# Macaron block on one core: ScalarE sums the last 128 queries of every second group in the score bank

## The chip, the cores and the metric

The kernel runs on one core of a Trainium2 chip. The metric is device time in microseconds of that core, from the start of the program to its end. Before the change it was 814.96 us (median of 3 runs, 813.83 to 816.62).

## The reference

Sixteen sequences of 512 tokens with 128 features (fp32) pass through a half feed-forward step, an attention, and a second half feed-forward step, each with a layer norm in front and a residual around it:

```
x = x + 0.5 * ffn(layernorm(x))
x = x + attn(layernorm(x))
x = x + 0.5 * ffn(layernorm(x))
```

The feed-forward is linear: a 128x128 weight rounded to int4 steps, a bias, and a low-rank term. The attention has 16 heads; keys and values come from a latent of 32 features, and the query weights are folded with the key weights, so each head's score is a product over 32 features. It is causal, with a softmax over the keys:

```
attn = softmax(where(key <= query, q @ k / 8, -inf))
y = attn @ v;  out = y @ Wout
```

## The kernel before, in words

Heads are worked on in groups of four (32 features each fill 128 partitions), four groups a sequence; two groups g and g + 1 form a pair. There are 32 pairs, each of five steps: STEP lists for each step a kind and, for kinds 0 and 1, which group of the pair it is for. Kind 0 is the last 128 queries (against 512 keys), kind 1 the third 128 queries with the first, kind 2 the second 128 queries of both groups. The last step of a pair is kind 0 of the odd group, g + 1.

A step n of the main loop (line 975) is a *burst* on TensorE (`burst`, line 673 on): it makes scores `sx` (queries on partitions) for the current pair, into two tiles of two PSUM banks each, and, six steps behind (LAG), transposed scores `tx` (keys on partitions) for the pair before, into four single banks. The `sx` are only there to find each query's maximum: DVE reduces them (`find_maxima`, lines 642 and 646, to `nmax`). POOL splits the maxima into three bf16 terms (lines 719 to 723), TensorE turns them (`mt`), ScalarE writes them out as `rows` (line 730), and TensorE adds them to the `tx`. ScalarE then takes the exponentials from `tx` to `pt` (line 655), and POOL zeroes what the mask forbids (line 668).

`merge` interleaves two streams of matmuls by their length: the first half of a burst writes two of the `tx` banks and the first `sx` tile, the second half the other two and the second `sx` tile. PSUM has eight banks: `ps_t` rotates over four single ones, `ps_s` over two double ones. After a burst, other products take the next single banks (`take`): the value products `o` (`values`, copied by ScalarE to `osb`, line 773), the sums `s`, the turned maxima, the query products `qt_ps` and so on. The next burst takes the banks after these.

The softmax's denominators need sums over keys, which lie on partitions of `pt`. POOL first adds the key blocks of a group (`add_01` line 738, `add_2` line 743, `add_23` line 748: b01 holds query blocks 1 to 3 without their last part, b23 that of block 3); TensorE multiplies with ones (`sum_products`, `s` from `pt` and from the two `b` tiles); ScalarE copies `s` to `ssb` (line 787). Four transfers of 2 KB take the four heads' rows of 512 sums to DRAM, one brings them back spread over 128 partitions (line 792), DVE takes reciprocals (line 822), and further transfers (lines 824 and 827) bring them back repeated over 32 partitions as `rb`, with which POOL scales `osb` (line 830).

Transfers nearly all go through SyncE's queue, in program order. All engines work in program order; the order is written out by hand. `plan` puts the pieces of the generators `front` (first feed-forward, layer norm, transposed activations, keys `kt`, queries `qt` of a sequence two or three windows ahead) and `tail` (output product, second feed-forward) at steps listed in FRONT_STEPS, SECOND_STEPS, THIRD_STEPS, FOURTH_STEPS and TAIL_STEPS, relative to the sequence's window of ten steps; a fraction says whether a piece stands before the burst (.5), after it (.75, written -.25) or at the step's end (whole).

Of the kernel before, what the change touches and what calls it, by code (L numbers as in the profile page):

```python
# [11 lines left out]
F32 = mybir.dt.float32  # L12
BF16 = mybir.dt.bfloat16
AF = mybir.ActivationFunctionType
# [11 lines left out]
def macaron_kernel(  # L26
# [331 lines left out]
    def to_dram(src, name):  # L358

        there = dram.tile([L, D], F32, tag=f"blocks_{name[0]}", name=f"blocks_{name}", bufs=2)  # L360
        nc.sync.dma_start(there.rearrange("(t p) d -> p t d", p=P), src)
        return there
# [58 lines left out]
    def front(b, st):  # L421


        x_sb, z = xs.pop(b), zs.pop(b)
        na, nb = f"a{b}", f"b{b}"
        la = ln_of("a", b) if b > 2 else early["a", b]
        lb = ln_of("b", b) if b > 1 else early["b", b]
        ln_stats(x_sb, la, "a", (0, 1))
        yield
        ln_stats(x_sb, la, "a", (2, 3))  # L430
        if b > 1:
            yield
        if 0 < b < B - 1:
            xs[b + 1] = load_x(b + 1)
            zs[b + 1] = load_blocks(x[b + 1], f"a{b + 1}")
        yield
        if b == 0:
            xt = turn(x_sb, na, "xt_a")
            yield
        xb = with_bias(x_sb, na, nc.gpsimd if b > 1 else nc.vector)  # L440
        yield
        if b:
            xt = turn_blocks(z, na, "xt_a")
            yield
        x1 = st["x1"] = ffn(xt, la, xb, na, "x1", 5)
        yield
        ln_stats(x1, lb, "b", (0, 1))
        yield
        ln_stats(x1, lb, "b", (2, 3))
        yield  # L450
        xn = ln_scale(x1, nb, lb)
        if b:
            there = to_dram(xn, nb)
            yield
            z = load_blocks(there, nb)
        yield
        xnt = turn_blocks(z, nb, "xnt_b") if b else turn(xn, nb, "xnt_b")
        yield
        mp = take(f"kt_ps_{b}")
        kt = st["kt"] = act2.tile([P, L], F32, tag="kt", name=f"kt_{b}", bufs=3)  # L460
        if b == 0:
            product(mp, wkv4_flat, xnt)
            nc.vector.tensor_copy(kt, mp)
        else:

            for j in range(NT):
                nc.tensor.matmul(
                    mp[ts(j, LD), :P], lhsT=wkv4_flat[:, :LD], rhs=xnt[:, ts(j, P)], start=True, stop=True,
                    skip_group_check=True,
                )  # L470
            kt4 = act2.tile([P, P], F32, tag="kt4", name=f"kt4_{b}", bufs=1)
            nc.vector.tensor_copy(kt4, mp[:, :P])
            yield
            kt_d = dram.tile([P, P], F32, tag="kt_d", name=f"kt_d_{b}", bufs=2)
            nc.sync.dma_start(kt_d, kt4)
            yield
            for h in range(HG):
                nc.sync.dma_start(
                    kt[ts(h, LD), :].rearrange("c (j n) -> c j n", j=NT), kt_d.rearrange("(j c) n -> c j n", j=NT)
                )  # L480

        def query(g):
            mp = take(f"qt_ps_{b}_{g}")
            product(mp, wqk_flat[:, ts(g, P)], xnt)
            if g % 2 == 0:
                st["qt", g] = act2.tile([P, 2, L], F32, tag="qt", name=f"qt_{b}_{g}", bufs=4)
            nc.scalar.copy(st["qt", g - g % 2][:, g % 2, :], mp)  # L487

        yield
        query(0)  # L490
        yield
        query(1)
        yield
        query(2)
        yield
        query(3)
        yield
# [8 lines left out]

    FRONT_STEPS = (-31, -30.5, -29, -28, -21, -19.25, -16, -16, -13, -10.5, -8, -4.25, -4, -3.5, -2, -1, 3, 4)
    SECOND_STEPS = (-9.5, -8.5, -7, -5.5, -5, -4.25, -4, -3.5, -2, -1, 3, 4)  # L510
    THIRD_STEPS = (-18.5, -18.5, -18.5, -18, -17.5, -17.25, -16, -16) + FRONT_STEPS[8:]
    FOURTH_STEPS = (-27, -26, -25.5, -25) + FRONT_STEPS[4:]
    TAIL_STEPS = (1.75, 2.5, 2.75, 3.5, 4.5, 7, 7, 7.75, 10.5)
    NORMALISED_STEPS = (5, 6)

    def tail(b, st, late=False):


        x2 = io.tile([P, NT, D], F32, tag="x2", name=f"x2_{b}")
        nm = f"c{b}"  # L520
        ln = ln_tile(nm) if late else ln_of("c", b)
        for half in (0, 1):
            yp = take(f"yp_{b}_{half}")[:, : 2 * D]
            for t in (0, 1):
                for g in range(NG):
                    product(yp[:, ts(t, D)], st["ot"][:, g, ts(2 * half + t, P)], wvo[:, g, :],
                            t == 0 and g == 0, g == NG - 1)
            nc.vector.tensor_tensor(
                x2[:, ts(half, 2), :], yp.rearrange("p (t d) -> p t d", d=D), st["x1"][:, ts(half, 2), :], ALU.add
            )  # L530
            if half and not late:
                there = to_dram(x2, nm)
            yield
            ln_stats(x2, ln, "c", (2 * half, 2 * half + 1))
            yield
        if late:
            xt = turn(x2, nm, "xt_c")
            yield
            ln_rstd(ln, "c")
            yield  # L540
            ln_newton(ln, "c")
        else:
            z = load_blocks(there, nm)
            yield
        xb = with_bias(x2, nm, nc.gpsimd)
        yield
        if not late:
            xt = turn_blocks(z, nm, "xt_c")
            yield
        x3 = ffn(xt, ln, xb, nm, "x3", 3)  # L550
        if not late:
            yield
        nc.sync.dma_start(out[b].rearrange("(t p) d -> p t d", p=P), x3)
        yield
# [80 lines left out]
    def find_maxima(sx, st, g, kind, u, pair):  # L635
# [9 lines left out]
        else:  # L645
            nc.vector.tensor_reduce(  # L646
                nmax[:, 1, heads, :], sx.rearrange("p k (u n) -> p k u n", u=2), AX.X, ALU.max, negate=True
            )

    def exponentials(tx, st, g, kind, u, pair):  # L650

        pt = probabilities(st, g + (u if kind < 2 else 0), kind)
        if isinstance(tx, list):
            for k in range(2):
                nc.scalar.activation(  # L655
                    pt[:, :, 2 * pair + k, :], tx[k].rearrange("p (b n) -> p b n", n=P), AF.Exp
                )
        else:
            nc.scalar.activation(
                pt[:, :, ts(pair, 2), :].rearrange("p b k n -> p k b n"),  # L660
                tx.rearrange("p k (b n) -> p k b n", n=P), AF.Exp,
            )
# [10 lines left out]
    def burst(n, s_at, t_at):  # L673
# [16 lines left out]
        for k in range(2):  # L690
            find_maxima(ss[k], *s_at, *s_kind, 1 - k)
            if t_at:
                exponentials(tt[k], *t_at, *t_kind, k)
        if n % STEPS == STEPS - 1:
            maxima(*s_at)
        if t_at:
# [34 lines left out]

    def add_01(st, g, k):

        if k == 0:
            st["b01", g] = probs.tile([P, 3, HG, P], F32, tag="b01", name=f"b01_{st['b']}_{g}")
        flat = [t.rearrange("p b k n -> p (b k n)")[:, ts(k, 6 * P)] for t in (
            st["b01", g], st["pt", 0, g][:, 1:], st["pt", 1, g][:, 1:])]
        nc.gpsimd.tensor_tensor(*flat, ALU.add)  # L738

# [4 lines left out]

    def add_23(st, g, u):

        both = st["b23", g + u] = probs.tile([P, HG, P], F32, tag="b23", name=f"b23_{st['b']}_{g + u}")
        nc.gpsimd.tensor_tensor(both, st["pt", 2, g][:, 2 + u], st["pt", 1, g + u][:, 0], ALU.add)  # L748

# [25 lines left out]
    def sum_products(st, g, u, s_ps):  # L775
        g1, w = g + u, ones_f[:, :LD]
        blocks(s_ps[:, :P], w, st["pt", 0, g1][:, :1], start=True)
        blocks(s_ps[:, P:], w, st["b01", g1])
        blocks(s_ps[:, 384:], w, st["b23", g1].unsqueeze(1))

    def sums(st, g, u):

        b, g1 = st["b"], g + u
        s_ps = take(f"s_{b}_{g1}")
        sum_products(st, g, u, s_ps)
        ssb = act2.tile([P, L], F32, tag="ssb", name=f"ssb_{b}_{g1}", bufs=3)
        nc.scalar.copy(ssb, s_ps)
        sums_d = dram.tile([HG, L], F32, tag="sums", name=f"sums_{b}_{g1}")
        for h in range(HG):
            nc.sync.dma_start(sums_d[h : h + 1], ssb[h * LD : h * LD + 1, :])  # L790
        st["sums", g1] = small.tile([P, HG * L // P], F32, tag="sum", name=f"sum_{b}_{g1}")
        nc.sync.dma_start(st["sums", g1], sums_d.rearrange("h n -> (h n)").rearrange("(p n) -> p n", p=P))

# [79 lines left out]
    early["a", 2] = early["b", 1]  # L873
    first, second = front(0, states[0]), front(1, states[1])
    masks()
    wmax = largest_of_rows()
    next(first)
    next(first)
# [95 lines left out]

    for n in range(N * STEPS):
        parts(n - 0.5)
        ready_work(n)
        burst(n, at(n), at(n, LAG))
        if due(n, 8):
# [124 lines left out]
```

## Time and profile before

| | |
|---|---|
| median of 3 runs | 814.96 us |
| the profiled execution's own time | 814.67 us |
| its span in the profile | 812.9 us |
| granted TensorE clock, mean | 0.989 |
| exponentials `pt`, 128x512 (ScalarE) | 616, mean 598 ns |
| maxima `nmax` of 128x1024 (DVE) | 128 on line 642, mean 1223 ns |
| POOL's add of 128x768 and of 128x512 (lines 738, 748) | 1821 ns and 1277 ns |
| POOL, busy | 678.4 us (83%) |

The profile is one execution. Its page gives busy times of the engines, the chain of work that ended last, and groups of instructions by line with a mean duration. The timeline lists instructions in order of time (start, duration, engine, line, what it writes and reads, how many); the waits list which engine waited for which, in total, how often and the longest. Matmul rows overlap each other: the distance from one start to the next says what a matmul costs TensorE.

### The profile page before, as it was taken

The numbers are of one execution on the slowest core, as the hardware profiler recorded it, in microseconds if no ns is written. First come the engines' busy times: TensorE is split into PE (matmuls) and PEld (weight loads), VectorE is DVE, ScalarE is ACT, GpSimd is POOL, SyncE is SP. The second block draws the span as 40 slices with busy tenths as digits, with TensorE's granted clock in tenths as the row PEclk, the third lists the DMA queues.
The fourth block names the chain that finished last, engine by engine and source line by source line (L and its number), as shares of the span: only waits on it lengthen the run. The fifth ranks groups of instructions, "written<-read, shape, count | busy, mean of one in ns | idle before, by whom it ended". The sixth has DMA issues, their size and how long they took to land.

```text
span 812.9 us, 35716 instructions
## 1 busy us (share of the span) xinstructions
PE 786.7 (97%) x15400; PEld 506.9 (62%) x15400; DVE 618.6 (76%) x1317; ACT 488.9 (60%) x971; POOL 678.4 (83%) x676
## 2 busy tenths in 40 slices
PE   7899999999999999999999999999999999999986
PEld 5456566675666657666566766666666766666554
DVE  7787887978779687877869787777878677686716
ACT  1237675757567565756667566666757566575651
POOL 1018898998998999898989989898999989998991
PEclk9989999999999999999999999999999999999998
DMA  5123122232422323332232323223222222212111
GB/s 138 27 57 68 32 72 60 69 71 73 95 61 69 77 66 80 76 82 60 70 84 61 84 69 82 67 67 88 56 64 67 51 72 69 59 46 59 41 41 30
DMA packets 171022, 54.01 MB, mean 66 GB/s; under 512 B 119512, under 2 KB 162680, under 8 KB 170864
## 3 DMA queue, kind: packets, MB, share of 16 engines
q1 hardware_dynamic: 170096, 51.44, 27.1%
q8 instruction: 120, 1.97, 1.0%
q14 instruction: 38, 0.31, 0.1%
q10 hardware_dynamic: 768, 0.30, 0.1%
HBM read 37.90 MB, written 13.80 MB: 64 GB/s over the span
## 4 chain that ended last, share of the span: by engine, by line
PE 75%; POOL 7%; DVE 7%; ACT 4%; DMA 4%; issue 2%; SPq 1%; DVEq 0%; POOLq 0%
PE sx L632 18%; PE tx L632 14%; PE o L754 14%; PE s L754 8%; PE yp L385 7%; PE qt_ps L385 6%; POOL b L738 4%; DVE nmax L642 3%; PE fp_a L385 2%; DMA rb<-recs 2%; ACT xn_b L355 2%; PE fp_c L385 2%; POOL ot L830 1%; DMA recs<-rec 1%; POOL b L743 1%
## 5 line engine op out<-in xcount | busy, mean ns | idle before, releaser
L642 DVE TENSOR_REDUCE nmax<-sx 128x2 f32<-128x768 f32 (+2 forms) x384 | 313.0, 863 | 106.4 <-PE tx L632 66.0
L655 ACT ACTIVATE pt<-tx 128x512 f32<-128x512 f32 x616 | 319.5, 598 | 85.5 <-PE tx L632 79.3
L632 PE MATMUL sx<-kt,qt 32*128 32x512 f32 (+3 forms) x2048 | 324.5, 444 | 0.0
L632 PE MATMUL tx<-qt,kt 32*128 32x512 f32 x1728 | 319.3, 469 | 0.0
L738 POOL TENSOR_TENSOR b<-pt,pt 128x768 f32<-128x768 f32 x126 | 226.8, 1821 | 0.5
L632 PEld LDWEIGHTS sx<-kt,qt 32*128 32x128 f32 x2048 | 176.7, 186 | 25.1 <-issue 1.0
L668 POOL TENSOR_SCALAR_AFFINE_SELECT pt<-pt 128x1024 f32<-128x1024 f32 (+1 forms) x162 | 145.2, 900 | 24.1 <-ACT pt L655 21.0
L754 PE MATMUL o<-pt,lat 128*32 128x512 f32 x1984 | 146.4, 435 | 0.9 <-POOL pt L668 0.9
L632 PEld LDWEIGHTS tx<-qt,kt 32*128 32x128 f32 x1728 | 131.5, 185 | 5.1
L754 PEld LDWEIGHTS o<-pt,lat 128*32 128x32 f32 x1984 | 62.5, 109 | 78.0 <-issue 57.7
L632 PE MATMUL tx<-rows,ones_u 6*128 6x512 bf16 (+1 forms) x988 | 109.9, 297 | 1.0 <-DVE wvo L292 0.5
L646 DVE TENSOR_REDUCE nmax<-sx 128x4 f32<-128x1024 f32 x64 | 75.4, 1219 | 32.1 <-PE tx L632 32.0
L830 POOL TENSOR_TENSOR ot<-osb,rb 128x512 f32<-128x512 f32 x62 | 79.0, 1274 | 20.3 <-DMA rb<-recs 20.3
L632 PEld LDWEIGHTS <-ones_u 6*128 6x128 bf16 x1024 | 43.2, 92 | 82.8 <-issue 70.1
L773 ACT COPY osb<-o 128x512 f32<-128x512 f32 x62 | 36.3, 585 | 92.3 <-PE o L754 92.3
L632 PE MATMUL sx<-eye_b,mask_w 32*128 32x64 bf16 (+1 forms) x2560 | 87.8, 183 | 2.9 <-DVE nmax L646 1.9
L632 PEld LDWEIGHTS <-mask_w 32*128 32x128 bf16 x2560 | 67.4, 92 | 33.0 <-issue 25.1
L743 POOL TENSOR_TENSOR b<-b,pt 128x512 f32<-128x512 f32 x63 | 80.5, 1277 | 5.1
L748 POOL TENSOR_TENSOR b<-pt,pt 128x512 f32<-128x512 f32 x63 | 80.4, 1277 | 0.1
L487 ACT COPY qt<-qt_ps 128x512 f32<-128x512 f32 x64 | 37.5, 586 | 53.8 <-PE qt_ps L385 53.8
L754 PE MATMUL s<-b,ones_f 128*32 128x384 f32 x992 | 65.1, 380 | 3.5 <-POOL b L743 3.5
L385 PE MATMUL qt_ps<-xnt_b_b,wqk 128*32 128x512 f32 x512 | 68.2, 605 | 0.1
(193 smaller groups left out, 813.8 us busy)
## 6 DMA issues: line engine op xcount, KB each, us to landing
rb<-recs SPq DMA_DIRECT2D x248, 64.0 KB
x<-in_x_dram SPq DMA_DIRECT2D x16, 256.0 KB
sums<-ssb SPq DMA_DIRECT2D x248, 2.0 KB
z_a<-in_x_dram SPq DMA_DIRECT2D x60, 64.0 KB
blocks_b<-xn_b SPq DMA_DIRECT2D x15, 256.0 KB
z_b<-blocks_b SPq DMA_DIRECT2D x60, 64.0 KB
kt<-kt_d SPq DMA_DIRECT2D x60, 64.0 KB
out_dram<-x_c SPq DMA_DIRECT2D x15, 256.0 KB
```

The source lines that it names most:

```text
L385: nc.tensor.matmul(dst[ts(h, LD), :], lhsT=w[:, ts(h, LD)], rhs=mv, start=start, stop=stop, skip_group_check=True)
L487: nc.scalar.copy(st["qt", g - g % 2][:, g % 2, :], mp)
L632: nc.tensor.matmul(dst, lhsT=w, rhs=mv, start=first, stop=last, skip_group_check=True)
L642: nc.vector.tensor_reduce(nmax[:, i, heads, u], sx[:, :, col : col + (i + 1) * P], AX.X, ALU.max, negate=True)
L646: nc.vector.tensor_reduce(nmax[:, 1, heads, :], sx.rearrange("p k (u n) -> p k u n", u=2), AX.X, ALU.max, negate=True)
L655: nc.scalar.activation(pt[:, :, 2 * pair + k, :], tx[k].rearrange("p (b n) -> p b n", n=P), AF.Exp)
L668: nc.gpsimd.affine_select(diag, diag, pattern=[[0, diag.shape[1]], [1, P]], compare_op=ALU.is_ge, fill=0.0, base=0, channel_multiplier=-1,)
L738: nc.gpsimd.tensor_tensor(*flat, ALU.add)
L743: nc.gpsimd.tensor_tensor(b01, b01, st["pt", 2, g][:, u], ALU.add)
L748: nc.gpsimd.tensor_tensor(both, st["pt", 2, g][:, 2 + u], st["pt", 1, g + u][:, 0], ALU.add)
L754: nc.tensor.matmul(dst[ts(h, LD), :].rearrange("p (b n) -> p b n", n=P), lhsT=w[h] if isinstance(w, list) else w, rhs=mv, start=start, sto ...
L830: nc.gpsimd.tensor_tensor(turned(st)[:, g, :], st["osb", g], st["rb", g], ALU.mult)
```

## The change

In the last step of each pair but the last one, ScalarE takes the exponentials of the `sx` tiles in place, with the negated maxima as the bias, and lets them be summed along the keys (`own_sums`): four ACTIVATEs of 128x512, one per head of the odd group, each with one sum per query. DVE turns the 128x32 tile that holds the sums (`own_sums_out`, seven steps after the pair began), and four transfers of 4 rows of 32 numbers take them to DRAM, where the odd group's sums of queries 384 to 511 are looked for. For that group `add_23` and the matmul on b23 fall away, `add_01` adds 4 instead of 6 blocks in each of its two instructions, the matmul on b01 has 256 instead of 384 columns, and `ssb` and its transfers have 384.

Besides, pieces of `front` and `tail` move: the transfer of `xn` (and that of `x2`) becomes a piece of its own; the key product (`kt_ps`) and `fp_a` now stand after the burst of a pair's last step, ahead of `o`; the query products move from there to other steps; the transpose `xt_a` stands ahead of the burst of a pair's last step.

```diff
-    FRONT_STEPS = (-31, -30.5, -29, -28, -21, -19.25, -16, -16, -13, -10.5, -8, -4.25, -4, -3.5, -2, -1, 3, 4)
-    SECOND_STEPS = (-9.5, -8.5, -7, -5.5, -5, -4.25, -4, -3.5, -2, -1, 3, 4)
+    FRONT_STEPS = (-31, -30.5, -29, -28, -22, -21.25, -16, -16, -13, -11.5, -10.5, -8, -6.25, -5.5, -4.5, -4, -2, 1, 3)
+    SECOND_STEPS = (-9.5, -8.5, -7, -6.25, -5.5, -5, -4.25, -4, -3.5, -2, -1, 1, 3)
...
-    TAIL_STEPS = (1.75, 2.5, 2.75, 3.5, 4.5, 7, 7, 7.75, 10.5)
+    TAIL_STEPS = (1.75, 2.5, 2.75, 3.5, 3.5, 4.5, 7, 7, 7.75, 10.5)
...
+    def own_sums(sx, st, g, pair):
+
+        st["own", g + 1] = own[g // 2 % 2]
+        for k in range(2):
+            nc.scalar.activation(
+                sx[:, k, :], sx[:, k, :], AF.Exp, bias=st["nmax", g][:, 3, 2 * pair + k, 1:2],
+                accum_out=st["own", g + 1][:, 2 * pair + k : 2 * pair + k + 1],
+            )
+
+    def own_sums_out(st, g):
+        sums_d = st["sums_d", g + 1] = dram.tile([HG, L], F32, tag="sums_0", name=f"sums_{st['b']}_{g}", bufs=3)
+        turned_ = small.tile([P, LD], F32, tag="own_t", name=f"own_t_{st['b']}_{g}", bufs=2)
+        nc.vector.transpose(turned_, st["own", g + 1])
+        for j in range(HG):
+            nc.sync.dma_start(sums_d[:, 384 + LD * j : 384 + LD * (j + 1)], turned_[j * LD : j * LD + HG, :])
...
+        if n % STEPS == STEPS - 1 and s_at is not groups[N - 1]:
+            for k in range(2):
+                own_sums(ss[k], *s_at, 1 - k)
         if n % STEPS == STEPS - 1:
             maxima(*s_at)
...
+        n_ = (4 if ("own", g) in st else 6) * P
...
     def add_23(st, g, u):
 
+        if ("own", g + u) in st:
+            return
...
+        if ("own", g1) in st:
+            blocks(s_ps[:, P:384], w, st["b01", g1][:, :2])
+            return
         blocks(s_ps[:, P:], w, st["b01", g1])
         blocks(s_ps[:, 384:], w, st["b23", g1].unsqueeze(1))
...
+        n_ = 384 if ("own", g1) in st else L
+        nc.scalar.copy(ssb[:, :n_], s_ps[:, :n_])
...
+            nc.sync.dma_start(sums_d[h : h + 1, :n_], ssb[h * LD : h * LD + 1, :n_])
...
     for n in range(N * STEPS):
         parts(n - 0.5)
+        if due(n, STEPS + 2, 0):
+            own_sums_out(*due(n, STEPS + 2, 0))
         ready_work(n)
         burst(n, at(n), at(n, LAG))
```

More of the change, by code (lines that the diff above doesn't have):

```diff
@@ L452, in front @@
         if b:
+            yield
             there = to_dram(xn, nb)
@@ L530, in tail @@
             )
-            if half and not late:
-                there = to_dram(x2, nm)
             yield
@@ L542, in tail @@
         else:
+            there = to_dram(x2, nm)
+            yield
             z = load_blocks(there, nm)
@@ L732, in add_01 @@
     def add_01(st, g, k):
+        n_ = (4 if ("own", g) in st else 6) * P
         if k == 0:
             st["b01", g] = probs.tile([P, 3, HG, P], F32, tag="b01", name=f"b01_{st['b']}_{g}")
-        flat = [t.rearrange("p b k n -> p (b k n)")[:, ts(k, 6 * P)] for t in (
+        flat = [t.rearrange("p b k n -> p (b k n)")[:, ts(k, n_)] for t in (
             st["b01", g], st["pt", 0, g][:, 1:], st["pt", 1, g][:, 1:])]
@@ L786, in sums @@
         ssb = act2.tile([P, L], F32, tag="ssb", name=f"ssb_{b}_{g1}", bufs=3)
-        nc.scalar.copy(ssb, s_ps)
-        sums_d = dram.tile([HG, L], F32, tag="sums", name=f"sums_{b}_{g1}")
+        n_ = 384 if ("own", g1) in st else L
+        nc.scalar.copy(ssb[:, :n_], s_ps[:, :n_])
+        sums_d = st["sums_d", g1] if n_ < L else dram.tile([HG, L], F32, tag="sums", name=f"sums_{b}_{g1}")
         for h in range(HG):
-            nc.sync.dma_start(sums_d[h : h + 1], ssb[h * LD : h * LD + 1, :])
+            nc.sync.dma_start(sums_d[h : h + 1, :n_], ssb[h * LD : h * LD + 1, :n_])
         st["sums", g1] = small.tile([P, HG * L // P], F32, tag="sum", name=f"sum_{b}_{g1}")
@@ L875, in macaron_kernel @@
     masks()
+    own = [const.tile([P, LD], F32, tag=f"own{i}", name=f"own{i}") for i in range(2)]
+    for tile_ in own:
+        nc.gpsimd.memset(tile_, 0.0)
     wmax = largest_of_rows()
```

## The prediction

> **What bounds the kernel now.** I read the page first, then the waits of TensorE, then two pairs of groups in the timeline.
>
> ```profile
> span 812.9 us, 35716 instructions
> ...
> PE 786.7 (97%) x15400; PEld 506.9 (62%) x15400; DVE 618.6 (76%) x1317; ACT 488.9 (60%) x971; POOL 678.4 (83%) x676
> ...
> PE 75%; POOL 7%; DVE 7%; ACT 4%; DMA 4%; issue 2%; SPq 1%; DVEq 0%; POOLq 0%
> ```
>
> TensorE is busy nearly all the time and carries three quarters of the chain that ended last. The gaps are few: over the whole run TensorE's largest waits for other engines outside head and tail are
>
> ```profile
> PE s L754 <- POOL b L743: 3.5, 7, 1.0
> ...
> PE sx L632 <- DVE nmax L642: 1.0, 3, 0.5
> ```
>
> So a microsecond taken off TensorE's stream, or added between its matmuls, moves the end by a microsecond; ScalarE's 40% of idle time helps only where TensorE doesn't wait for ScalarE. The change puts work there, in the last of a pair's five steps. This is that step in the timeline (start, duration, engine, line, groups; the first row begins its burst at 416.61):
>
> ```profile
> 416.61 0.23 PE L632 MATMUL tx<-rows,ones_u 6*128 6x128 bf16 x2
> 417.88 2.43 DVE L642 TENSOR_REDUCE nmax<-sx 128x2 f32<-128x1024 f32 x2 [0.84 <-PE tx L632]
> 418.02 2.06 ACT L655 ACTIVATE pt<-tx 128x512 f32<-128x512 f32 x4 [0.69 <-PE tx L632]
> 418.86 2.36 PE L754 MATMUL o<-pt,lat 128*32 128x512 f32 x32
> 421.03 1.04 PE L385 MATMUL qt_ps<-xnt_b_b,wqk 128*32 128x512 f32 x8
> 421.28 0.58 ACT L773 COPY osb<-o 128x512 f32<-128x512 f32 x1 [1.20 <-PE o L754]
> 422.01 0.39 PE L632 MATMUL tx<-rows,ones_u 6*128 6x512 bf16 x2
> 423.07 0.38 PE L632 MATMUL tx<-rows,ones_u 6*128 6x512 bf16 x2
> ```
>
> The next burst starts at 422.01 and needs its first half of banks; 1.06 us later it needs the second half. All eight banks are in rotation (four single, two double): of the second half one single bank is the one that `o` used, free once ScalarE has copied `osb`; the double one is the second score tile of the step before, free today when DVE's maxima end at 420.31.
>
> **What goes.** POOL: for the odd group two adds shrink from 768 to 512 columns (1821 to 1277 ns) and the add of 1277 ns goes: 2 x 0.544 + 1.277 = 2.37 us a pair, 73 us for 31 pairs. Only POOL's lateness counts. From start to start, `s` takes 0.6 to 0.8 us more than its usual 1.20 where it waits; over all windows this sums to 4.0 us. In the tail three gaps of TensorE (770.2, 774.0, 779.2; 0.95 + 0.94 + 1.02 = 2.9 us) follow POOL's chain. I credit both: 6.9 us.
>
> TensorE: `s` of the odd group loses 256 of 640 columns. I price them by spacing:
>
> ```profile
> 410.42 0.40 PE L754 MATMUL s<-pt,ones_f 128*32 128x128 f32 x8
> 410.63 1.05 PE L754 MATMUL s<-b,ones_f 128*32 128x384 f32 x16
> 411.61 0.28 PE L632 MATMUL tx<-rows,ones_u 6*128 6x256 bf16 x2
> ```
>
> 128 columns take 0.21 us to the next start, so 256 save 0.43 us: x 31 = 13.3 us. Busy time would credit 0.40 (24.9 us over 62 groups) + 0.20 (51.6 less 38.9 us over 62) = 0.60 us, 18.6 us in all. [...] Gains: 13.3 + 6.9 = 20.2 us.
>
> **What comes.** Per pair four ACTIVATEs on 128x512 in the score bank. The order of instructions puts them on ScalarE between the step's four `pt` exponentials and `osb`; the second of each two also carries a wait for ScalarE's own semaphore, that is, for the first to end. Their length: `pt` takes 598 ns, without a bias tile. These rows give the tile and the wait (426.56 has a bias tile, 426.90 has none and waits for the row before it):
>
> ```profile
> 426.56 0.32 ACT L338 ACTIVATE y_w<-mv_w,eps 128x12 f32<-128x12 f32 x1
> 426.90 0.21 ACT L339 ACTIVATE y_w<-y_w 128x12 f32<-128x12 f32 x1
> ```
>
> The tile costs 0.10 us, so d = 0.70 us (0.60 if it hides). Waiting for its own engine leaves no overlap and 0.03 us between; otherwise neighbours overlap by 0.10 us (four `pt` in 2.06 us). Reading the sum out, r, is in no row. It is extra work behind the ACTIVATE on the same engine, so not below 0; a whole short ACTIVATE took 0.21 us, or 0.32 us with a tile. The nearest row is the 0.21 us one; overlapped it would be 0.11 us. I take r = 0.15 us and keep 0 to 0.32. The chain of four is C = 4(d + r) - 0.04 = 3.36 us (2.36 to 4.04).
>
> Even-numbered last steps (kind A; times from the burst's start T): `pt` ends at 3.47, so the first sum starts at 3.37; maxima are ready at 2.5 and 3.70, before they are asked for. Queued behind the sums is `osb`, 0.585 us, overlapped by 0.10, with 0.06 us to hand over: the bank is free at 3.37 + C + 0.545. The rescheduled `front` puts the key product (428.03 to 428.42: 0.39 us) ahead of `o` (2.27 us to the next burst) and moves `qt` away; the burst itself takes 2.24 us to the next start (438.64 to 440.88). So the next burst starts at 4.90 and needs the bank at 5.96. TensorE stands still for C - 2.05 = 1.31 us. The other kind (B) has `fp_a` (403.22 to 404.11: 0.9 us) ahead of `o`: burst at 5.41, bank needed at 6.47. But there DVE is late. Before:
>
> ```profile
> 439.16 1.24 DVE L504 STREAM_TRANSPOSE lat<-kt 32x128 f32<-32x128 f32 x4
> 440.44 2.35 DVE L642 TENSOR_REDUCE nmax<-sx 128x2 f32<-128x1024 f32 x2
> 442.82 0.71 DVE L366 STREAM_TRANSPOSE xt_a_a<-z_a 128x512 f32<-128x512 f32 x1
> ```
>
> The maxima start 1.80 us after their burst (438.64), and the change puts the 0.65 us transpose ahead of them: first maxima at 1.80 + 0.65 + 1.21 + 0.06 = 3.72, where the sums start. Stall: 3.72 + C + 0.545 - 6.47 = C - 2.205 = 1.155 us. The first pair has nothing else on ScalarE and stalls nowhere: 15 of each kind, 19.7 + 17.3 us. The last three such steps have neither key product nor `fp_a` as cover: 0.39 + 2 x 0.9 = 2.2 us more. Together 39.2 us.
>
> What costs here is the banks' late release. [...]
>
> At nothing I count: DVE's transpose of 128x32 (between nothing and the 0.30 us of a 32x128 one; DVE is 24% idle; in its step a 0.28 us copy leaves the queue; without that cover 0.3 us for half the pairs, 5 us); the four short transfers (some 1.2 us of SP's queue a pair, like `sums`; behind them stand the odd group's `sums`, wanted a step later; were they late, POOL's product and not TensorE would wait); 0.11 us less for `ssb`.
>
> Sum: 814.67 us (profiled execution: span 812.9 + 1.8 around it) - 20.2 + 39.2 = 833.7 us; that execution is 0.3 us under the runs' median of 814.96.
>
> **Rivals.**
> Short chain: the bias tile hides and the sum comes out free (d = 0.60, r = 0, C = 2.36). Stalls 0.31 and 0.155 us, 15 x 0.465 + 2.2 = 9.2 us against 20.2: 804 us, faster. It decides below C = 2.73, that is 0.69 us for each sum with its read-out. For it: POOL's and TensorE's savings are certain; against: the 0.10 us of the tile and the wait on its own engine are both in rows.
>
> Long chain: the read-out costs like the 0.32 us row (C = 4.04): stalls 1.99 and 1.835 us, 57.4 + 2.2 = 59.6 us, 854 us. For it: it follows its ACTIVATE and can't overlap it. Against: it moves one element.
>
> The bank isn't on the path: TensorE finds enough to do ahead of it, and only the gains remain, 795 us. Against: matmuls stand in program order behind the one that waits.
>
> **How the numbers follow.** Forecast (r 0.05 to 0.25) 0.58, long chain 0.15, short chain 0.20 including its neighbourhood of no change, bank off the path 0.07. Of the short chain 0.07 lands within 0.3% (2.4 us, about what a measurement of this kernel can tell from no change). Faster 0.20, same 0.07, slower 0.73. The range leaves out the fastest case, half of the short chain's faster part and the far end of the long chain: 806 to 850.
>
> **What would show it.** Right: four ACTIVATE rows a pair of about 0.7 us into `sx`, plus a small read-out; a gap of about 1.2 us on TensorE in the middle of each pair's first burst, ended by ScalarE's `osb`; `s` from b in 0.43 us less; POOL busy near 605 us with idle time it had not; the wait of `s` for POOL gone. Wrong: no such gap, or one ended by DVE or a DMA; or a sum with its read-out under 0.69 us.

## The result, and the profile after

After the change the kernel took 825.46 us (median of 4 runs, 823.86 to 825.85); the kernel before, run beside it, 815.07 us (813.83 to 816.62). The ratio is 1.0123, 95% interval 1.0101 to 1.0145: slower by 10.4 us. The prediction said 833.7 us within 806 to 850, so its direction and its range held, and its size was 8 us too large. The profiled execution of after took 825.85 us.

The page of after: its span, the engines' busy times, the granted TensorE clock in 40 slices, and the shares of the chain that ended last.

```profile
span 824.0 us, 35625 instructions
...
PE 787.2 (96%) x15152; PEld 499.1 (61%) x15152; DVE 616.1 (75%) x1348; ACT 573.5 (70%) x1219; POOL 608.6 (74%) x647
...
PEclk9969999999999999999999999999999999999997
...
PE 65%; ACT 17%; DVE 9%; POOL 3%; issue 2%; DMA 2%; SPq 1%; DVEq 0%; ACTq 0%; POOLq 0%
```

Before, the chain had 75% on TensorE and 4% on ScalarE. Now 17% of it is on ScalarE, though that engine is busy for only 70% of the span: its work is late in a few places, not too much in all. POOL lost 70 us of work and its share of the chain fell from 7% to 3%. The third slice of the clock, about 41 to 62 us, has a 6 that we come back to.

TensorE's waits for other engines in after (total us, times, longest):

```profile
PE tx L633 <- ACT osb L796: 9.2, 17, 0.5
PE fp_a L385 <- DVE xt_a_a L366: 3.1, 11, 0.3
...
PE sx L633 <- ACT sx L655: 2.2, 2, 1.9
```

The first is the wait that the prediction was built on. The second and third are in none of its sums. The wait of `s` for POOL, which headed this list before, is gone.

The new groups of ScalarE (busy us, mean ns of one):

```profile
L655 ACT ACTIVATE sx<-sx,nmax 128x512 f32<-128x512 f32 x124 | 81.9, 661 | 4.5 <-DVE nmax L643 2.4
...
L655 ACT ACTIVATION_READ_ACCUMULATOR sx<-sx,nmax 128x1 f32 x124 | 24.4, 197 | 0.0
```

Reading the sum out is an instruction of its own with 197 ns. The timeline shows what that costs. Here is one pair's last step of kind A (key product ahead of `o`); its burst began at 423.43:

```profile
426.01 2.36 PE L777 MATMUL o<-pt,lat 128*32 128x512 f32 x32
...
426.75 0.67 ACT L655 ACTIVATE sx<-sx,nmax 128x512 f32<-128x512 f32 x1
...
427.32 0.21 ACT L655 ACTIVATION_READ_ACCUMULATOR sx<-sx,nmax 128x1 f32 x1
...
427.57 0.66 ACT L655 ACTIVATE sx<-sx,nmax 128x512 f32<-128x512 f32 x1
...
428.25 0.65 ACT L655 ACTIVATE sx<-sx,nmax 128x512 f32<-128x512 f32 x1
...
428.31 0.39 PE L633 MATMUL tx<-rows,ones_u 6*128 6x512 bf16 x2
...
429.05 0.66 ACT L655 ACTIVATE sx<-sx,nmax 128x512 f32<-128x512 f32 x1
...
429.73 0.58 ACT L796 COPY osb<-o 128x512 f32<-128x512 f32 x1
...
430.35 0.37 PE L633 MATMUL tx<-rows,ones_u 6*128 6x512 bf16 x1 [0.54 <-ACT osb L796]
```

`o` ends near 428.37, but ScalarE copies it only at 429.73, behind four sums. From the first sum to `osb` it is 2.98 us. The starts of the sums are 0.82, 0.68 and 0.80 us apart: the second of each two works on the same double bank and waits for the first to end, which costs 0.14 us (0.82 less 0.68). The read-out overlaps both neighbours, so it adds some 0.12 us, not 0.20 (0.68 less 0.66, and 0.10 for the overlap that neighbours have without it, as the `pt` before the change, four of 598 ns in 2.06 us). The next burst starts at 428.31; its second half, wanted 1.06 us later, gets `o`'s bank at 430.35. That is a stall of 0.98 us from start to start. (The bracket says 0.54, since rows of matmuls overlap; the waits view counts in the same way and shows less than the time lost.)

Kind B (`fp_a` ahead of `o`), whose burst began at 398.35:

```profile
400.09 0.71 DVE L366 STREAM_TRANSPOSE xt_a_a<-z_a 128x512 f32<-128x512 f32 x1
...
400.72 2.32 DVE L643 TENSOR_REDUCE nmax<-sx 128x2 f32<-128x1024 f32 x2
...
400.94 1.08 PE L385 MATMUL fp_a<-w_mid,xt_a_a 128*32 128x128 f32 x32 [0.28 <-DVE xt_a_a L366]
...
401.94 0.66 ACT L655 ACTIVATE sx<-sx,nmax 128x512 f32<-128x512 f32 x1 [0.15 <-DVE nmax L643]
...
404.91 0.57 ACT L796 COPY osb<-o 128x512 f32<-128x512 f32 x1
...
405.17 0.74 PE L633 MATMUL tx<-rows,ones_u 6*128 6x512 bf16 x2
```

Here `fp_a` itself waits for DVE's transpose `xt_a`: 2.59 us from the burst's start where 2.24 is usual. Everything behind it moves by this 0.35 us, and so the burst waits for the bank only 0.36 us.

### The profile page after: what moved, and what is told of

Read it like the earlier page. It is cut to its first block, busy times and chain, and to the rows that moved or that the text cites. A ratio compares the mean times of both kernels' runs of the same rounds, so it can differ in the third digit from the quotient of the medians.

```text
span 824.0 us, 35625 instructions
## 1 busy us (share of the span) xinstructions
PE 787.2 (96%) x15152; PEld 499.1 (61%) x15152; DVE 616.1 (75%) x1348; ACT 573.5 (70%) x1219; POOL 608.6 (74%) x647
## 4 chain that ended last, share of the span: by engine, by line
PE 65%; ACT 17%; DVE 9%; POOL 3%; issue 2%; DMA 2%; SPq 1%; DVEq 0%; ACTq 0%; POOLq 0%
PE sx L633 16%; PE tx L633 12%; PE o L777 11%; ACT pt L672 7%; PE yp L385 7%; ACT sx L655 6%; PE s L777 6%; PE qt_ps L385 5%; PE fp_a L385 2%; PE fp_c L385 2%; ACT xn_b L355 2%; DVE x_c L397 2%; DVE lat L505 1%; DVE nmax L643 1%; POOL b L759 1%
## 5 line engine op out<-in xcount | busy, mean ns | idle before, releaser
L672 ACT ACTIVATE pt<-tx 128x512 f32<-128x512 f32 x616 | 323.7, 598 | 73.9 <-PE tx L633 70.9
L633 PE MATMUL sx<-kt,qt 32*128 32x512 f32 (+3 forms) x2048 | 334.0, 449 | 0.0
L633 PE MATMUL tx<-qt,kt 32*128 32x512 f32 x1728 | 328.0, 475 | 0.0
L759 POOL TENSOR_TENSOR b<-pt,pt 128x768 f32<-128x768 f32 (+1 forms) x126 | 193.2, 1556 | 0.5
L633 PE MATMUL tx<-rows,ones_u 6*128 6x512 bf16 (+1 forms) x988 | 120.8, 298 | 10.4 <-ACT osb L796 9.2
L857 POOL TENSOR_TENSOR ot<-osb,rb 128x512 f32<-128x512 f32 x62 | 79.1, 1277 | 41.0 <-DMA rb<-recs 29.3
L777 PEld LDWEIGHTS o<-pt,lat 128*32 128x32 f32 x1984 | 64.8, 109 | 71.9 <-issue 55.5
L633 PEld LDWEIGHTS <-mask_w 32*128 32x128 bf16 x2560 | 69.6, 93 | 37.6 <-issue 25.9
L655 ACT ACTIVATE sx<-sx,nmax 128x512 f32<-128x512 f32 x124 | 81.9, 661 | 4.5 <-DVE nmax L643 2.4
L385 PE MATMUL yp<-wvo,ot 128*32 128x128 f32 x1920 | 58.8, 274 | 0.5 <-POOL ot L857 0.5
```

The source lines that it names most:

```text
L385: nc.tensor.matmul(dst[ts(h, LD), :], lhsT=w[:, ts(h, LD)], rhs=mv, start=start, stop=stop, skip_group_check=True)
L633: nc.tensor.matmul(dst, lhsT=w, rhs=mv, start=first, stop=last, skip_group_check=True)
L655: nc.scalar.activation(sx[:, k, :], sx[:, k, :], AF.Exp, bias=st["nmax", g][:, 3, 2 * pair + k, 1:2], accum_out=st["own", g + 1][:, 2 * pa ...
L672: nc.scalar.activation(pt[:, :, 2 * pair + k, :], tx[k].rearrange("p (b n) -> p b n", n=P), AF.Exp)
L777: nc.tensor.matmul(dst[ts(h, LD), :].rearrange("p (b n) -> p b n", n=P), lhsT=w[h] if isinstance(w, list) else w, rhs=mv, start=start, sto ...
L857: nc.gpsimd.tensor_tensor(turned(st)[:, g, :], st["osb", g], st["rb", g], ALU.mult)
```

## The experiments

All comparisons are with the kernel before, run on the same chip; after is 1.0123. The theory: the four sums stand ahead of `osb`, TensorE waits for `o`'s bank, and the rest is paid by `xt_a` and by the first pair. The first rival: the moved pieces of `front` and `tail` cost the time. The second: the four short transfers do.

**e1_no_exps** leaves the four ACTIVATEs out: the denominators of those queries come from a constant, and the rest of the change stays.

```diff
-            nc.scalar.activation(sx[:, k, :], sx[:, k, :], AF.Exp, ...)
+            pass
...
-        nc.gpsimd.memset(tile_, 0.0)
+        nc.gpsimd.memset(tile_, 1.0)
```

> The changed kernel with its four ACTIVATEs a pair left out (the tile of sums holds ones, so queries 384 to 511 of the odd groups are divided by wrong sums); the turn, the short transfers, the moved pieces and the smaller sums all stay. Theory (ScalarE's four sums hold osb and the score banks, and TensorE waits in the pair's first burst): the 22.6 us of waiting in those bursts and the 3.9 us at the start go, the wait of fp_a for its transpose (4.6 us) stays: 799 us, 796 to 803. Rival 1 (the moved pieces cost the time): 815 to 825 us. Rival 2 (turn and transfers cost it): 815 to 825 us.

Measured: 802.48 us, ratio 0.9833 (0.9782 to 0.9883). The first of its waits, and the one for POOL:

```profile
PE fp_a L385 <- DVE xt_a_a L366: 3.5, 11, 0.4
...
PE s L774 <- POOL b L761: 2.1, 2, 1.1
```

The wait for `osb` is gone, and the sums with all that they cause cost 23.0 us (825.46 less 802.48). What they replace is worth 12.9 us, less than the 20.2 us of the prediction: the wait for `xt_a` is there without any sum (4.7 us from start to start), and the tail gave back less than the 2.9 us credited.

**e2_steps_only** is the kernel before with the moved pieces alone (the step lists, the transfers as pieces of their own).

```diff
-    FRONT_STEPS = (-31, -30.5, -29, -28, -21, -19.25, -16, -16, -13, -10.5, -8, ...
+    FRONT_STEPS = (-31, -30.5, -29, -28, -22, -21.25, -16, -16, -13, -11.5, -10.5, -8, ...
```

> The kernel before, with nothing but the moved pieces of front and tail. Theory: at most the wait of fp_a for its transpose comes in, 4.6 us: 815 to 820 us. Rival 1: most of the loss, 825 us or more. Rival 2: 815 us.

Measured: 823.8 us, ratio 1.0103 (1.0071 to 1.0136), a miss. Its first two waits:

```profile
PE s L755 <- POOL b L744: 6.8, 11, 1.6
PE fp_a L385 <- DVE xt_a_a L366: 3.5, 11, 0.3
```

From start to start `fp_a` loses 4.8 us, and `s` 9.0 us behind POOL where it lost 4.0 before: 9.8 us together, against 8.4 us in the medians (9.8 in the spans). So the moved pieces alone are not free. But the second part shows only while POOL has its old load.

**e3_own_old_steps** is the other half: after with the steps of before.

```diff
-    FRONT_STEPS = (-31, -30.5, -29, -28, -22, -21.25, -16, -16, -13, -11.5, -10.5, -8, ...
+    FRONT_STEPS = (-31, -30.5, -29, -28, -21, -19.25, -16, -16, -13, -10.5, -8, ...
```

> The changed kernel with the pieces where they stood before. In the pair's last step o and qt_ps then both wait behind the sums on ScalarE: osb ends 6.9 us after the burst's start and qt 7.4 us, wanted at 6.5 us. Theory: 0.9 us of waiting in each of 30 bursts, about 28 us, as much as the changed kernel pays in bursts and before fp_a together: 823 to 829 us. Rival 1: the loss goes with the moved pieces, 795 to 805 us. Rival 2: 825 us.

Measured: 829.59 us, ratio 1.0171 (1.0129 to 1.0214), as expected, with this first of its waits:

```profile
PE tx L632 <- ACT osb L795: 8.1, 30, 0.3
```

All 30 bursts now wait, about 1 us each (29.4 us from start to start). The moved pieces save 4 us where the sums are, and cost 8 us where they are not. The first rival has a part in the loss, but it is not what the sums cost.

**e4_twice_out** makes the four short transfers twice, the second time to a place that nobody reads.

```diff
+            nc.sync.dma_start(again[:, LD * j : LD * (j + 1)], turned_[j * LD : j * LD + HG, :])
```

> The changed kernel with the four short transfers doubled: each pair sends the same 4 x 4 rows once more, to a tile in DRAM that nobody reads. Theory: nobody on TensorE's path waits for SP's queue here: 825 us, within 2. Rival 2: as much again as the transfers cost now, 5 us or more: 830 us and above. Rival 1: 825 us.

Measured: 823.65 us, ratio 1.01 (1.0059 to 1.0141): no slower than after. The second rival is out; the transfers were rightly counted at nothing. (DVE's turn of the sums was not doubled, but e1 has it too, and is fast.)

**e5_no_first** leaves the first pair as it was before.

```diff
-        if n % STEPS == STEPS - 1 and s_at is not groups[N - 1]:
+        if n % STEPS == STEPS - 1 and t_at and s_at is not groups[N - 1]:
...
-        if due(n, STEPS + 2, 0):
+        if due(n, STEPS + 2, 0) and n > STEPS + 2:
```

> The changed kernel without the four sums in the first pair of the run, where no transposed scores are made yet (that group is summed the old way). Theory: the wait of 1.9 us for the sums at the run's start goes, and with it the second stretch at half clock that follows it: 3.9 us less than the changed kernel's 825.5: 821 to 822 us. If the stretch at half clock comes of something else, 823.5 us.

Measured: 822.8 us, ratio 1.0083 (1.0051 to 1.0114); its span is 2.0 us shorter than after's. The interval overlaps after's, so the price of the first pair rests on the traces. The rows of after that e5 lacks:

```profile
51.94 0.27 PE L633 MATMUL sx<-eye_b,mask_w 32*128 32x32 bf16 x8 [1.94 <-ACT sx L655]
...
53.42 0.27 PE L633 MATMUL sx<-eye_b,mask_w 32*128 32x32 bf16 x8 [0.26 <-ACT sx L655]
```

The first pair has no `tx` yet, and its next scores go into the very bank whose sums ScalarE is still taking. Then the clock falls. Windows of after (span; busy us and instructions of PE, PEld, DVE, ACT, POOL; granted clock; DMA share; GB/s):

```profile
52.00:56.00 4.00, 3.74 (x52) 1.73 (x55) 3.44 (x10) 2.35 (x7) 1.94 (x4) 0.79 0.58 105
56.00:60.00 4.00, 4.00 (x44) 2.74 (x38) 2.17 (x5) 1.76 (x6) 0.00 (x0) 0.50 0.53 97
60.00:64.00 4.00, 3.94 (x84) 2.93 (x78) 3.93 (x9) 2.85 (x6) 0.64 (x1) 0.86 0.06 18
```

The same windows of e5:

```profile
52.00:56.00 4.00, 3.59 (x51) 1.73 (x52) 3.75 (x13) 1.02 (x4) 2.24 (x6) 1.00 0.47 75
56.00:60.00 4.00, 3.61 (x74) 2.56 (x72) 3.83 (x10) 2.80 (x6) 0.64 (x1) 1.00 0.63 128
60.00:64.00 4.00, 3.73 (x75) 2.37 (x68) 3.74 (x5) 3.70 (x10) 2.08 (x2) 1.00 0.31 89
```

After runs at half clock (0.50) for 6.8 us here, from 54.29 to 61.12 us, and e5 (1.00 in all three) doesn't. (An earlier stretch, 40.6 to 47.5 us in after, is in before as well, where the windows 40 to 44 and 44 to 48 us have 0.55 and 0.60; in e5 the third slice of the page, which holds it, has the 8 that before has.) From the burst ahead of the stall to the fourth one behind it after takes 19.2 us (47.71 to 66.89), e5 16.4 (48.10 to 64.46) and before 16.7 (47.47 to 64.13). So the first pair costs 2.5 us against before: 1.7 behind the stall, where `qt_ps` takes 3.00 us to the next burst in place of 1.32, and 0.8 in the slow stretch. The 3.9 us of the expectations compares the burst at 77.10 us with that of before at 73.20, and in after an `fp_a` (0.87 us) already stands ahead of that burst. In e5 that group's `s` takes its 0.43 us again.

**e6_out_sbuf** writes the exponentials, which nobody reads, to an idle tile in SBUF instead of the score bank. The second of each two then has no reason to wait for the first.

```diff
-                sx[:, k, :], sx[:, k, :], AF.Exp, ...
+                wq_sb[:, ts(k, 4), :].rearrange("p t n -> p (t n)"), sx[:, k, :], AF.Exp, ...
```

> The changed kernel with the exponentials written to an idle tile in SBUF in place of the score bank; the second of two no longer waits for the first to end. Theory (the length of the chain on ScalarE is what TensorE waits for): 2 x 0.14 us less chain, so 0.28 us less of each of 30 waits, 8.4 us: 817 us, 815 to 819. If the chain's length isn't what counts, 825 us; if ScalarE writes slower to SBUF than to PSUM, 820 us or above.

Measured: 815.53 us, ratio 0.9989 (0.9972 to 1.0006): no difference from before, and 10 us under after. The group, and the wait:

```profile
L655 ACT ACTIVATE wq_sb<-sx,nmax 128x512 f32<-128x512 f32 x124 | 83.6, 694 | 2.8 <-DVE nmax L643 2.1 <-issue 0.7
```

```profile
PE tx L633 <- ACT osb L796: 5.7, 17, 0.4
```

One ACTIVATE is longer (694 ns against 661), and yet the four are over sooner, since their starts are 0.66 us apart throughout. The stall of kind A falls from 0.98 to 0.69 us, that of kind B from 0.36 to 0.07: 8.5 us over all bursts (22.4 less 13.9). In the head, e6 runs at half clock for 3.4 us where after has 6.8 (0.69 and 0.88 in the windows 52 to 56 and 56 to 60 us, 1.00 in the third), and 46.73 to 64.41 us is 1.5 us shorter than the same stretch of after. The two make the 10 us. So writing the exponentials back into the bank, where the second of two waits for the first, costs about as much as the whole change loses. For the single instruction the bank was the faster destination here, by 33 ns (661 against 694); for the chain of two in one bank the wait of 0.14 us is dearer.

**e7_osb_dve** takes `osb` of the even groups to VectorE, out of the sums' way.

```diff
-            nc.scalar.copy(st["osb", g + u], o_ps)
+            if u == 0:
+                nc.vector.tensor_copy(st["osb", g + u], o_ps)
+            else:
+                nc.scalar.copy(st["osb", g + u], o_ps)
```

> The changed kernel with the copy osb of the even groups, the one that stands behind the sums, on DVE. Theory (the last to come is osb, the score bank is next): the wait in the one kind of burst falls from 0.98 to about 0.5 us (the fourth sum's read-out ends 1.5 us after the burst's start, the bank is wanted at 1.07), in the other from 0.36 us to nothing: 13 us less, 812 us, 810 to 816. If the score bank came last already, 825 us; if DVE's maxima become late by the copy, 818 us or above.

Measured: 823.87 us, ratio 1.0095 (1.0064 to 1.0126): a miss. The bursts waited as much less as expected (kind A 0.49 us, kind B nothing), but TensorE's first wait is now

```profile
PE s L777 <- POOL b L764: 9.0, 9, 1.7
```

and POOL's first is this one, which in after was 29.3 us:

```profile
POOL ot L860 <- DMA rb<-recs: 76.8, 28, 4.1
```

12.8 us were freed in the bursts, but 11.8 us are lost in `s`, and `fp_a` loses 6.1 us where it lost 4.2 in after. The path: the reciprocal `rec` is queued on VectorE behind the copy and the statistics, its transfers and then `rb` come late, POOL's product `ot` waits for `rb`, and the adds for `s` are queued behind `ot`.

**e8_all_mended** puts e5, e6 and e7 together and turns `xt_a` 2.5 steps earlier.

```diff
-    FRONT_STEPS = (-31, -30.5, -29, -28, -22, -21.25, ...
+    FRONT_STEPS = (-31, -30.5, -29, -28, -24.5, -21.25, ...
```

> All three of these, and the transpose xt_a issued 2.5 steps earlier (ahead of the second burst of the pair, where DVE has idle time). Theory: waits of 0.2 us in one kind of burst and none in the other, none of fp_a, none at the start: 825.5 - 15 x 1.14 - 4.6 - 3.9 = 800 us, 797 to 806, below both kernels. If the savings on POOL and TensorE are smaller than thought, 808 us or above.

Measured: 820.56 us, ratio 1.0067 (1.0032 to 1.0102): a miss. The wait of `fp_a` is gone and the bursts lose 4.6 us in all, but the path of e7 takes it back:

```profile
PE s L777 <- POOL b L764: 14.8, 13, 2.1
```

Some of the loss is the clock's: behind five of the six longest of these stalls the trace shows some 3.4 us at half clock (the windows of 8 us in which these begin have a clock of 0.79 to 0.88). Two windows about one of them, with TensorE busy for 2.23 of 4 us and then a clock of 0.57:

```profile
440.00:444.00 4.00, 2.23 (x52) 1.25 (x48) 3.23 (x4) 2.10 (x4) 3.92 (x5) 1.00 0.18 40
444.00:448.00 4.00, 4.00 (x60) 3.10 (x60) 1.29 (x2) 2.84 (x8) 4.00 (x4) 0.57 0.17 48
```

**e9_three_mends** is e8 with `osb` left on ScalarE.

```diff
-            if u == 0:
-                nc.vector.tensor_copy(st["osb", g + u], o_ps)
-            else:
-                nc.scalar.copy(st["osb", g + u], o_ps)
+            nc.scalar.copy(st["osb", g + u], o_ps)
```

> After with three mends, osb left on ScalarE: the exponentials go to an idle SBUF tile, the first pair does without own sums, and xt_a is turned 2.5 steps earlier. Where the three prices are separate and nothing else becomes late: 815.5 (the SBUF version) less 2 to 2.7 (first pair) less 4.6 (TensorE's feed-forward product that starts late behind xt_a) = 808 to 809, range 806 to 812, with the waits of TensorE for xt_a gone and s waiting for POOL about as in after. The rival: what is freed is given back where POOL's product ot waits for its transfer rb and the sums' second term is queued behind it, as with osb on VectorE: 814 to 817, and TensorE's s waits for POOL 5 us or more.

Measured: 811.25 us, ratio 0.9942 (0.9924 to 0.9961). This beats both kernels, before by 0.6% and after by 1.7%, though it is 2 to 3 us behind the sum of its parts. `s` does not wait for POOL, nor `fp_a` for `xt_a`. The burst of kind B lost part of its gain (0.15 us each instead of 0.07, and 14.8 us over all bursts), since `o` no longer comes late behind `fp_a`. And the first pair was worth less than the 2 to 2.7 us put in: 46.71 to 63.71 us is only 0.7 us shorter than the same stretch of e6, whose slow stretch was already the shorter one, and that group's `s` takes 0.43 us more.

**e10_osb_dve_rec** tests the path of e7: e7 with the reciprocals ahead of the copy.

```diff
         burst(n, at(n), at(n, LAG))
+        recips(n)
...
-        for u in range(2):
-            if due(n, 6 + 2 * u):
-                st, g = due(n, 6 + 2 * u)
-                reciprocals(st, g + u)
```

> As the version with osb of the even groups on VectorE (823.9), but each step's reciprocal of the sums is put on VectorE right behind that step's maxima, ahead of the osb copy and the normalisation's statistics. If that version lost its gain because the reciprocal came late behind them, and with it the transfers of rb, POOL's ot and the sum b, then TensorE's s waits for POOL falls from 11.9 us (start to start) to 2 to 4 and the time is 814 to 817. If the lateness comes from the transfers' own queue, or from the copy's length on VectorE ahead of the maxima, the time stays at 821 to 825.

Measured: 816.94 us, ratio 1.0003 (0.9984 to 1.0023), as expected. `s` lost 0.2 us from start to start, and POOL's wait is

```profile
POOL ot L860 <- DMA rb<-recs: 14.7, 19, 1.6
```

So the late reciprocal was the cause in e7. Not all is won: TensorE's bursts lose 17.2 us instead of 9.5, with waits for VectorE's copies and for `x_a` ahead of them.

**e11_all_mended_rec** is e8 with the same edit as e10.

> The version with all four mends (820.6), with the reciprocals put right behind the maxima as well. By the theory that the late reciprocal makes POOL late: s waiting for POOL falls from 17.8 us to 2 to 5, time 803 to 809. By the rival (transfers' queue, or VectorE's copy itself): 818 to 822.

Measured: 810.75 us, ratio 0.9924 (0.9901 to 0.9948): 9.8 us under e8, against 12 to 18 expected, so it misses its range; `s` gained 16.5 us and the bursts lost 8.2, of which 2.4 in the one at 488.88 us, which waits 1.8 us for `x_a` and `osb` on VectorE. The mean granted clock of its profiled execution was 0.987, that of e9's 0.991. Its time can't be told from e9's.

**e12_one_behind_osb** is e9 with the fourth sum issued behind `osb`.

```diff
-            for k in range(2):
-                own_sums(ss[k], *s_at, 1 - k)
+            own_sums(ss[0], *s_at, 1)
+            own_sums(ss[1], *s_at, 0, (0,))
+            last.append(lambda: own_sums(ss[1], *s_at, 0, (1,)))
...
+        while last:
+            last.pop()()
         turn_maxima(n)
```

> The version with three mends (811.25), with the fourth of the own sums issued behind osb instead of ahead of it, so that three of 0.66 us stand ahead and one behind. By the theory that the sums cost by standing ahead of osb on ScalarE: in the 15 bursts of kind A the chain ends 0.66 us earlier, the stall of 0.69 us each goes, and the time falls by up to 10 us, to 801 to 806. If the score bank that the fourth sum reads is then missed by the next burst's second half of scores, which starts about 1.1 us into that burst, half of it is given back: 805 to 809. By the rival that what is freed in these bursts is given back elsewhere, or that the stall is not due to the order on ScalarE: 810 to 813.

Measured: 814.74 us, ratio 0.9994 (0.9981 to 1.0007): slower than e9, worse than every case I had written down. The step of kind A:

```profile
422.73 0.61 ACT L799 COPY osb<-o 128x512 f32<-128x512 f32 x1
...
423.19 0.73 ACT L655 ACTIVATE wq_sb<-sx,nmax 128x512 f32<-128x512 f32 x1
...
423.36 0.40 PE L633 MATMUL tx<-rows,ones_u 6*128 6x512 bf16 x2
...
424.07 0.70 PE L633 MATMUL sx<-kt,qt 32*128 32x512 f32 x2 [0.31 <-ACT wq_sb L655]
```

`osb` is early and the `tx` no longer wait for it. But the matmuls of the second score tile wait for the fourth sum, which still reads that bank. Kind A loses 0.69 us as before, and kind B 0.37 instead of 0.15. The burst's second half wants two banks, and ScalarE works off both: the order only chooses which is late.

## Why the prediction was right, point by point

All terms in us of the profiled execution; the measured ones are from start to start, after against before.

| step of the prediction | predicted | measured |
|---|---|---|
| `s` of the odd group, 31 x 0.43 | -13.3 | -13.3 |
| `s` waiting for POOL | -4.0 | -3.9 |
| gaps in the tail | -2.9 | -1.2 |
| bursts behind the sums | +39.2 | +22.4 |
| `fp_a` waiting for `xt_a` | none | +4.2 |
| first pair | none | +2.5 |
| sum (span) | +19.0 | +10.7 (span: +11.1) |

The tail is measured from the first `tx_late` to the fourth (768.96 to 783.32 us before, 781.23 to 793.94 after), without the 0.43 us of its `s`, which the first row has. 0.4 us of the span is in none of these rows.

- **Right: the mechanism and its place.** The sums stand ahead of `osb`, the gap is in the middle of the next burst and ended by `osb`. e1 takes the sums away, and the gap goes; e7 takes `osb` out of their queue, and it halves. The last three such steps, which have less cover, lost 2.4 us more than the others of their kinds, forecast 2.2. The gain on TensorE's matmuls and the end of `s` waiting for POOL came as worked out (POOL busy 608.6 us, forecast 605).
- **Mis-sized: the chain.** C was 3.36 us, 3.26 up to the start of `osb`; that stretch measures 2.98. The ACTIVATE has 0.66 us, not 0.70: with SBUF as destination, like `pt`, it has 0.69 (e6), so the 0.10 us for the bias tile was right, and the bank as destination was the faster one. The read-out adds 0.12 us, not 0.15, although its row shows 0.20. The waits of the second of each two came as put in (starts 0.82 and 0.80 us apart, 0.68 without). This takes kind A from 1.31 to 0.98 us.
- **Mis-sized: kind B.** 1.155 us was forecast, 0.36 came. The shorter chain makes 0.28 of the difference, maxima that were ready 0.13 us sooner some more, and `fp_a`'s lateness 0.35.
- **Wrong: the cover in kind B.** The prediction put the transpose `xt_a` ahead of the maxima and counted what that does to the maxima. It didn't ask who else waits for it: `fp_a`, moved to stand right behind the burst, reads it. That is some 0.35 us in each of 11 places and less in two more, 4.2 us in all, and it is there in e1 and e2 without any sums. e9, with the transpose earlier, has no such wait.
- **Wrong: "The first pair has nothing else on ScalarE and stalls nowhere".** The wait listed there is 1.9 us, because its next scores want the bank of the sums at once, and a half-clock stretch follows. e5 shows both gone.
- **Mis-sized: the tail.** 1.2 us came of the 2.9 credited: two of the three gaps closed, the first grew from 0.95 us to 1.6 (`mt` waiting for POOL's `terms`), and a `yp` behind them took 0.4 us more.
- The two omissions add 6.7 us and the tail 1.7, and the oversized stalls take away 16.8; the error of the sum is the difference of larger ones, so part of its nearness is luck.
- **The rivals.** The long chain (4.04 us) and the short one (2.36 us) were both off; in e6 the chain is 2.65 us up to `osb`, so C is about 2.75, and the time comes out level with before; the prediction put the point of no change at C = 2.73. That it fell there is partly luck: at C = 2.75 the prediction's formulas give 0.70 us for kind A, which came (0.69), but 0.55 for kind B, where 0.07 came, and what was saved there went to `fp_a` and the first pair, which the formulas left out.

## What to carry to other kernels

A score bank that an extra reader holds, and a bank whose reader stands behind it on the same engine, were late together here (kind A lost 0.69 us with `osb` behind the fourth sum, e9, and ahead of it, e12): find which of the next burst's banks is wanted first, and price the chain up to its release, here with starts 0.66 us apart where the unused output went to SBUF and 0.82 where the second waited for the first in the bank. When a product is moved forward to cover a wait, check that its inputs are ready at the new place. When work is moved to another engine, look at what is queued behind it there; here a late reciprocal of 0.2 us made its transfers, POOL and then TensorE late (e7: 11.8 us lost in `s`, and 0.2 us in e10 with the reciprocal earlier).

## What the runs showed of the hardware

- A sum taken along with an ACTIVATE appears as a second instruction, ACTIVATION_READ_ACCUMULATOR, 197 ns with the bank as destination (213 ns with SBUF, e6), of which some 0.12 us is added to the pitch of a chain.
- After a stall of 1.9 us on TensorE in the head of after, the granted clock was half (0.50) for 6.8 us; in e6, with one of 1.8 us at the same place, it was 0.69 and 0.88 in the windows 52 to 56 and 56 to 60 us. On the pages, the third slice of the clock, which holds this place, has 6 or 7 in five runs with this stall (6 in after, e3 and e10, 7 in e4 and e6) and 8 in seven without it (before, e1, e2, e5, e9, e11, e12). In the loop of after, with its stalls of 1.4 us and less, the clock is full (1.00) from 61 us to 815 us. In e8 `s` stalled six times for 1.78 to 2.31 us, and five of these were followed by some 3.4 us at half clock: the windows of 8 us from 104, 200, 344, 440 and 632 us, in which TensorE is busy for 5.92 to 6.46 us, have a clock of 0.88, 0.85, 0.81, 0.79 and 0.79. The sixth, of 1.83 us, was not, nor were any of up to 1.45 us: between 80 and 784 us only the windows right behind the first three of those five are also below 1.00 (0.91, 0.94, 0.98). In e7, with two stalls of 1.93 and 1.97 us, all windows of 8 us from 80 to 784 us have 1.00. So the length of a stall alone does not settle it, and what does was not shown. In the trace of after, the stretches at half clock up to 815 us are 26.98 to 30.40, 40.64 to 47.46 and 54.29 to 61.12 us: 3.4, 6.8 and 6.8 us long.
